# Sorted-table lookups in a fused two-layer kernel: one comparison and a difference product, table products in pieces, the own tile in one operation

## The chip, the cores and the metric

One core of one Trainium2 chip. The metric is device microseconds of one execution; the median of several runs is the time of a kernel. Engines are called as in the profile: PE (TensorE), PEld (its weight loads), DVE (VectorE), ACT (ScalarE), POOL (GpSimd), SP (SyncE, which issues most DMAs).

## What is computed

Two layers on x of shape 2 x 256 x 64 x 64, float32, so N = 4096 tokens per batch:

```python
# layer 0
e   = prelu(bn(conv3x3(x)))            # 64 channels
sim = e.T @ e                          # N x N per batch
p   = sparsemax(sim, rows)             # max(sim - tau, 0)
x   = x + x @ p
# layer 1 (256 channels in, 128 inside)
g = g_w x + g_b;  a = w_t theta(x);  b = w_p phi(x)
f = relu(a[:, None] + b[None, :] + c)  # N x N
y = (f / N) @ g
x = x + bn(wz_w y + wz_b)
```

Layer 1 needs no N x N matrix where the tokens are sorted. f(i, j) is not zero only for those j whose b_j lies above -(a_i + c). With the tokens of a batch sorted by key b, y_i is a_i times a running sum of g plus a running sum of b g, both taken at one place of the sorted table. So layer 1 becomes: rank the keys, scatter rows (g, b) by rank, form running sums, and for each token find its place and fetch one row.

## The kernel before, in words

The executed path is `sparse_path` (L191 on). Nearly all of it is written as tasks of a list scheduler, `Plan` (L94 on): a task has a cost for each engine that may run it, a rank, tasks it comes after, a latency, and buffers that it takes or frees (`Ring`, `Hold`). `run` emits, again and again, the task that can begin first; among those that would start without delay `pick` takes the lowest rank. So the order on every engine is fixed when the kernel is built, by costs, due times and the rank constants of L281 (`R0`, `K0`, `CH0` for batch 0's ranking, `R1`, `K1`, `CH1` for batch 1's, `BE` for the counting products, `RW0`/`RW1` for the rows, `LS` for the lists, `DB`, `A0`, `G0` and so on). Each engine, and SP's queue of DMAs, then works in that order.

Layer 0, for each batch: the convolution (PE, `cv_in`/`cv_out`, L363); a survey of sim in tiles (PE `sv` L476, L508, ACT L528, DVE `xbs` L524), which lists the rows with more than one entry; for these rows the thresholds (DVE `mq` L777, ACT `z` L797 and DVE `z` L799); and the update `av` (PE L836), added into x by DVE L843. For four of the blocks POOL first multiplies x by a mask (L831; a `tick` L826/829 stands ahead). Layer 1's g, b and a come from `project` and `project_in` (PE `g` L873, L899; DVE `ga` L879, L906, L910).

Layer 1 is the class `Ranked`, twice. Batch 0 (r0) ranks all 32 tiles of 128 tokens. Batch 1 (r1) ranks 24 tiles; the other 8 tiles' part is computed directly (ACT `f` L1512, PE `py` L1520, ACT `rest` L1531). Its steps:

- `keys` (L1000 to 1014, DVE): the key per token, with two spare bits for a lower and an upper bound.
- `spread` (L939): PE turns the key column to a row (`pt_k` L924), ACT copies (`row_k` L928), SP stores it (`rd_k` L932) and loads it into all 128 partitions (`kb` L944). The same is done with a in pieces (`rd_a`, `ab`; `a_of_0` L1456 to 1462 for batch 0).
- `above(t)`: the keys of all columns from tile t on against tile t's keys, on ACT (Sign, L1050) or DVE (is_gt with a sum, L1054). The 0/1 matrix `junk` feeds PE `below` (L1065 and L1076), which counts along partitions for the later tiles; `below_out` (L1087) copies a row of it and `bt` (L1093) turns it.
- `ties(t)` (L1101, DVE): equal keys in the own 128 x 128 tile with a lower index.
- `place` (L1115 to 1120, DVE): the rank of four tiles; first for tiles 0 to 15, then for the others. `scatter` (L1126, POOL): one indirect DMA per tile into the sorted table `sg` in DRAM.
- `load` (L1141, SP) brings the sorted table back as `tab0`, `tab1`, and (L1143, L1144) the first key of the next partition as `nxt`. `products` (L1150 to 1153, DVE) makes b g; `sums` (L1160, DVE) the running sums within a partition; `po` (L1164, PE) and `raised` (L1167, DVE) add what lies before; `stored` (L1173, SP) writes the table `tb`.
- Lookups, for 8 blocks of 512 tokens: `limits` (L1177 to 1179) and `segments`, two DVE comparisons (L1187, L1188) that give a one-hot matrix of the partition in which each token's place lies; `pk` (PE L1196) reads that partition's keys out; `counts` (L1205 to 1208, DVE) counts within it.
- `fetch` (L1213, POOL): one indirect DMA per tile of 128 tokens, 32 in each batch; 16 fit the buffer `r`. `taken`: DVE L1226, PE `yr` L1233, then `yT` (ACT L1238, DVE L1240 in batch 1), PE `pz` (L960), DVE `x` (L964), and SP's store of the output (L967).

`begin` (L1255) and `chain` (L1305) write these as tasks.

Of the kernel before, what the change touches and what calls it, by code (L numbers as in the profile page):

```python
# [8 lines left out]
F32 = mybir.dt.float32  # L9
BF16 = mybir.dt.bfloat16  # L10
# [9 lines left out]
P = 128  # L20
# [14 lines left out]
TINY = 2.0**-60  # L35
STEEP = 2.0**40
# [154 lines left out]
def sparse_path(ctx: ExitStack, tc, a, out, rows_i):  # L191
# [89 lines left out]
    DB, CV1, LS, RW0, SV1, RW1, A0, G0, A1, R0, K0, CH0, R1, K1, CH1, P1, P2, SP1, PY, PF, BE = -15.47, 6.58, -12.34, -12.34, -12.37, -24.38, 6.88, -11.7, -0.72, -32.06, -0.3, 11.42, 11.12, 11.73, 6.58, -24.23, -0.6, 10.82, 17.06, 12.47, -12.07  # L281
# [698 lines left out]
    class Ranked:  # L980
# [43 lines left out]
        def turn(self):  # L1024
            self.a = small.tile([P, 2, NT], F32, name=f"a_{self.b}", tag=f"a{self.b}")
            nc.scalar.copy(self.a[:, 0], self.ga[:, :, CI + 2])
            nc.scalar.mul(self.a[:, 1], self.ga[:, :, CI + 2], -1.0)
# [8 lines left out]
        def above(self, t, on_act, d):  # L1036
# [11 lines left out]
            c = ds(t * P, n - t * P)  # L1048
# [49 lines left out]
        def ties(self, t):  # L1098

            junk = small.tile([P, P], BF16, name=f"tied_{self.b}_{t}", tag="tied", bufs=1)  # L1100
            nc.vector.scalar_tensor_tensor(  # L1101
                junk, self.kb[:, ts(t, P)], self.key[:, t : t + 1], low,
                ALU.is_equal, ALU.mult, accum_out=self.cnt[:, t, 2:3],
            )

        def place(self, t0, bt):
# [5 lines left out]
            for t in range(t0, t0 + 4):  # L1112
                known = t * P - sum(u in self.on_act for u in range(t)) * (P // 2)
                known += (R - t) * P // 2 if t in self.on_act else 0
# [21 lines left out]
        def load(self):  # L1136
# [5 lines left out]
            self.nxt = small.tile([P, 1], F32, name=f"nxt_{b}", tag=f"nxt{b}")  # L1142
            nc.vector.memset(self.nxt, -3.0e38)  # L1143
            nc.sync.dma_start(out=self.nxt[0 : P - 1], in_=sv[1:P, 0, CI + 1 : CI + 2])  # L1144

        def products(self, h):
            b, R, tab = self.b, self.R, self.tab[h]
            if h == 0:
                self.kr = small.tile([P, R + 1], F32, name=f"kr_{b}", tag=f"kr{b}")
                nc.vector.tensor_scalar_mul(self.kr[:, R : R + 1], lane, float(R))  # L1150
            t0, n = self.parts[h]
            nc.vector.tensor_copy(self.kr[:, ds(t0, n)], tab[:, :, CI + 1])
            nc.vector.tensor_mul(
                tab[:, :, CI + 1 : CS], tab[:, :, 0:CI], tab[:, :, CI : CI + 1].to_broadcast([P, n, CI])
            )
# [19 lines left out]
        def limits(self):  # L1175
            self.lim = small.tile([P, 2], F32, name=f"lims_{self.b}", tag=f"lims{self.b}")
            nc.vector.tensor_scalar_mul(self.lim[:, 0:1], self.kr[:, 0:1], -1.0)  # L1177
            nc.vector.memset(self.lim[0:1, 0:1], -3.0e38)
# [773 lines left out]
```

## Time and profile before

Three runs: 744.95, 740.04 and 737.0 us, median 740.04. The profiled execution took 744.85 us, of which the span from the first to the last instruction is 743.1; the mean granted clock of PE was 0.894. All times below are of that execution.

| | |
|---|---|
| PE, DVE, ACT, POOL busy | 601.1, 527.4, 322.3, 221.8 us |
| batch 0: keys written, on all partitions (first `junk`) | 374.3 to 376, 391.9 us |
| batch 0: first and last scatter | 437.7, 488.4 us (end) |
| batch 0: `x_7_1` (last L843), table load issued | 498.9, 490.1 us |
| batch 1: key row on all partitions (first DVE `junk`) | 523.1 us |
| batch 1: first and last scatter | 564.9, 598.6 us (end) |
| batch 0: table raised, first fetch | 590.6 to 599.3, 609.9 us |
| batch 1: table raised, first fetch | 642.7 to 649.3, 657.6 us |
| last fetch ends, last `x`, end of the span | 708.2, 733.5, 743.1 us |

How to read it: a line with the mark L1101 is line 1101 of the kernel; `a<-b` is written tile and read tiles; "busy, mean ns" is the sum and the mean of one. Rows by stage give the window, its length, the busy time of PE, PEld, DVE, ACT and POOL with the number of instructions, the granted clock, the DMA share and GB/s. A wait is put down to what ended last before the waiting instruction.

### The profile page before, as it was taken

The numbers are of one execution on the slowest core, as the hardware profiler recorded it, in microseconds if no ns is written. First come the engines' busy times: TensorE is split into PE (matmuls) and PEld (weight loads), VectorE is DVE, ScalarE is ACT, GpSimd is POOL, SyncE is SP. The second block draws the span as 40 slices with busy tenths as digits, with TensorE's granted clock in tenths as the row PEclk, the third lists the DMA queues.
The fourth block names the chain that finished last, engine by engine and source line by source line (L and its number), as shares of the span: only waits on it lengthen the run. The fifth ranks groups of instructions, "written<-read, shape, count | busy, mean of one in ns | idle before, by whom it ended". The sixth has DMA issues, their size and how long they took to land.

```text
span 743.1 us, 8392 instructions
## 1 busy us (share of the span) xinstructions
PE 601.1 (81%) x2829; PEld 286.6 (39%) x2835; DVE 527.4 (71%) x1074; ACT 322.3 (43%) x484; POOL 221.8 (30%) x290
## 2 busy tenths in 40 slices
PE   5998999999597999999877878766998876574562
PEld 4663444444332333435432233336543433341220
DVE  6966777777869877877589987016798627973551
ACT  0123575766376564772089863001796650000000
POOL 0119910000030402010304246820004737567510
PEclk9999999999789899999998978679799897578796
DMA  9621000110210000000230000153310193476541
GB/s 351 198 54 30 1 15 14 29 22 9 86 27 0 1 0 1 0 1 2 76 147 4 1 21 23 54 133 133 125 29 29 44 336 91 156 253 183 160 169 62
DMA packets 34268, 57.07 MB, mean 77 GB/s; under 512 B 12942, under 2 KB 21000, under 8 KB 33192
## 3 DMA queue, kind: packets, MB, share of 16 engines
q1 hardware_dynamic: 28440, 42.72, 17.1%
q0 software_dynamic: 5344, 13.14, 6.4%
q10 hardware_dynamic: 432, 0.59, 0.3%
q8 instruction: 24, 0.39, 0.2%
q14 instruction: 28, 0.23, 0.1%
HBM read 32.67 MB, written 21.66 MB: 73 GB/s over the span
## 4 chain that ended last, share of the span: by engine, by line
PE 59%; DVE 25%; issue 6%; another core or an unknown queue 3%; DMA 3%; ACT 2%; POOL 0%; DVEq 0%; SPq 0%; ACTq 0%
PE sv L476 14%; PE av L836 9%; PE py L1520 8%; PE cv_in L363 6%; PE cv_out L363 6%; DVE mq L777 3%; PE pz L960 3%; DVE junk L1054 3%; DVE tied L1101 2%; DVE x L964 2%; PE g L873 2%; PE g L899 2%; PE bt L1093 2%; DVE xbs L524 2%
## 5 line engine op out<-in xcount | busy, mean ns | idle before, releaser
L528 ACT ACTIVATE sv<-sv,nthr 128x1024 f32<-128x1024 f32 (+1 forms) x133 | 131.2, 986 | 99.3 <-PE sv L508 47.9
L524 DVE TENSOR_TENSOR xbs<-sv,xbs 128x1024 f32<-128x1024 f32 (+1 forms) x120 | 130.7, 1089 | 37.3 <-PE sv L476 30.3
L476 PE MATMUL sv<-e 64*128 64x512 f32 x512 | 136.3, 642 | 5.8 <-ACT sv L528 4.4
L836 PE MATMUL av<-z,xbs 128*128 128x512 f32 x192 | 114.0, 716 | 17.4 <-DVE x L843 8.8
L1126 POOL DMA_INDIRECT sg<-ga,rank x56 | 55.5, 990 | 79.2 <-DVE rk L1118 55.8
L1213 POOL DMA_INDIRECT r<-tb,k x64 | 65.5, 1024 | 44.1 <-issue 15.8
L1050 ACT ACTIVATE junk<-kb,bound 128x2816 bf16<-128x2816 f32 (+26 forms) x39 | 69.9, 1799 | 16.7 <-PE below L1076 8.7
L476 PEld LDWEIGHTS sv<-e 64*128 64x128 f32 x512 | 45.6, 195 | 72.2 <-issue 42.8
L836 PEld LDWEIGHTS av<-z,xbs 128*128 128x128 f32 x192 | 37.9, 221 | 78.7 <-issue 55.2
L1520 PE MATMUL py<-f,ga 128*128 128x512 f32 x128 | 67.7, 671 | 0.2 <-issue 0.2
L1233 PE MATMUL yr<-ident,r 128*128 128x128 f32 x64 | 16.8, 342 | 48.0 <-DVE r L1226 34.2
L363 PE MATMUL cv_out<-v,wu 128*64 128x256 f32 (+1 forms) x384 | 49.1, 395 | 7.6 <-DVE v L325 7.6
L1238 ACT ACTIVATE yT<-yr 128x512 f32<-128x512 f32 x8 | 4.8, 597 | 109.6 <-PE yr L1233 68.2
L446 POOL TENSOR_TENSOR sq<-es 128x512 f32<-128x512 f32 x8 | 8.9, 1111 | 133.4 <-ACT es L437 111.0
L363 PE MATMUL cv_in<-v,wu 128*64 128x256 f32 (+1 forms) x384 | 46.6, 382 | 1.0 <-ACT c L374 1.0
L843 DVE SCALAR_TENSOR_TENSOR x<-av,b,x 128x512 f32<-128x512 f32 x32 | 23.7, 747 | 32.6 <-PE av L836 19.4
L964 DVE SCALAR_TENSOR_TENSOR x<-pz,s,x 128x512 f32<-128x512 f32 x32 | 23.1, 746 | 31.8 <-remote 14.3
L960 PE MATMUL pz<-yT,wz_sb 128*128 128x512 f32 x64 | 39.5, 745 | 5.3 <-issue 1.9
L1054 DVE TENSOR_SCALAR_CACHE_REDUCE junk<-kb,ga 128x2688 bf16<-128x2688 f32 (+13 forms) x17 | 40.5, 2381 | 4.1 <-PE below L1076 3.7
L1512 ACT ACTIVATE f<-ab,ga 128x1024 f32<-128x1024 f32 x32 | 35.9, 1141 | 13.0 <-PE py L1520 7.3
L363 PEld LDWEIGHTS cv_out<-v,wu 128*64 128x64 f32 x384 | 28.4, 141 | 31.5 <-issue 14.2
L1520 PEld LDWEIGHTS py<-f,ga 128*128 128x128 f32 x128 | 25.8, 214 | 29.0 <-issue 28.7
(217 smaller groups left out, 859.4 us busy)
## 6 DMA issues: line engine op xcount, KB each, us to landing
out<-x SPq DMA_DIRECT2D x32, 256.0 KB
tb<-tab SPq DMA_DIRECT2D x3, 2056.0 KB
x<-in_x SPq DMA_DIRECT2D x8, 512.0 KB
tab<-sg SPq DMA_DIRECT2D x3, 1040.0 KB
x<-in_x SPq DMA_DIRECT2D x4, 544.0 KB
e<-e SPq DMA_DIRECT2D x16, 128.0 KB
et<-es SPq DMA_DIRECT2D x16, 128.0 KB
mask<-kd SPq DMA_DIRECT2D x2, 1024.0 KB
```

Source lines behind the costliest of these rows:

```text
L363: nc.tensor.matmul(d[jp, g][ts(h, CR), n, (r0 - r) * HH : (r1 - r) * HH], lhsT=taps(j, kc, dy), rhs=v[:, kc, r0 + dy - 1 : r1 + dy - 1], s ...
L476: nc.tensor.matmul(ps[:, ts(h, CB)], lhsT=lhs(h), rhs=e[ts(h, CR), q], start=True, stop=True)
L524: nc.vector.tensor_tensor(out=acc[:, cols], in0=d[i, q][:, cols], in1=acc[:, cols], op=ALU.max)
L528: nc.scalar.activation(ps, ps, AF.Relu, bias=both["nthr"][:, i : i + 1], accum_out=got_s["over"][:, i, q : q + 1])
L836: nc.tensor.matmul(pss[j, ct], lhsT=got["xb"][:, k, ts(ct, P)], rhs=got["zs"][k][:, ts(j, CB)], start=(k == 0), stop=(k == KB - 1),)
L960: nc.tensor.matmul(d["z"][:, ct], lhsT=wz_sb[:, ts(ct, P)], rhs=d["y"], start=True, stop=True)
L964: nc.vector.scalar_tensor_tensor(xc, d["z"][:, ct], s1[:, ct : ct + 1], xc, ALU.mult, ALU.add)
L1050: nc.scalar.activation(slot[:, c], kb[:, c], AF.Sign, scale=STEEP, bias=self.bound[:, 1, t : t + 1], accum_out=cnt[:, t, 3:4],)
L1054: nc.vector.tensor_scalar(slot[:, c], kb[:, c], self.key[:, t : t + 1], None, ALU.is_gt, ALU.add, accum_out=cnt[:, t, 1:2],)
L1126: rows = nc.gpsimd.indirect_dma_start(out=self.sg, out_offset=bass.IndirectOffsetOnAxis(ap=self.rank[:, t : t + 1], axis=0), in_=self.ga[: ...
L1213: nc.gpsimd.indirect_dma_start(out=self.r[:, t % TH], out_offset=None, in_=self.tb, in_offset=bass.IndirectOffsetOnAxis(ap=self.k[:, t : t ...
L1520: nc.tensor.matmul(pys[q][:, ts(h, CB)], lhsT=ga1[0][:, m, 0:CI], rhs=f[0][:, m % 4, ts(h, CB)], start=(m == NR), stop=(m == NT - 1),)
```

## The change

1. Lookups. One DVE comparison of a against a single limit writes a bf16 0/1 matrix `seg` (ring of two). PE multiplies it by a constant bf16 matrix, identity minus shifted identity, so that each partition's row has the next one's taken off (`one_segment`); ACT copies the result to `oh` (`one_segment_out`). `limits` has one column, and `nxt` with its memset and DMA is gone; the keys kept for `pk` have their sign turned; the count is limited by a `min`.
2. Table products are tasks of four tiles each: on ACT four operations of 128 x 128, or on DVE one of 128 x 512. The keys are copied apart from them (`keys_of`).
3. `ties` becomes `own`: key difference above a tiny negative step for lower indices, one operation. `above` starts at the next tile, 128 columns fewer, and the last tile needs none.
4. `turn` is one ACT copy instead of two.
5. The rank constants have new values, so the scheduler writes another order.

```diff
-    DB, CV1, LS, RW0, SV1, RW1, A0, G0, A1, R0, K0, CH0, R1, K1, CH1, P1, P2, SP1, PY, PF, BE = -15.47, 6.58, -12.34, -12.34, -12.37, -24.38, 6.88, -11.7, -0.72, -32.06, -0.3, 11.42, 11.12, 11.73, 6.58, -24.23, -0.6, 10.82, 17.06, 12.47, -12.07
+    DB, CV1, LS, RW0, SV1, RW1, A0, G0, A1, R0, K0, CH0, R1, K1, CH1, P1, P2, SP1, PY, PF, BE = -27.4, 6.58, -13.63, -19.99, -13.75, -12.96, -8.26, -8.17, -0.45, -1.13, -0.3, 6.13, 6.58, -7.96, -7.87, -19.68, -8.17, 6.43, 17.29, 6.88, -7.87
...
-            self.a = small.tile([P, 2, NT], F32, name=f"a_{self.b}", tag=f"a{self.b}")
-            nc.scalar.copy(self.a[:, 0], self.ga[:, :, CI + 2])
-            nc.scalar.mul(self.a[:, 1], self.ga[:, :, CI + 2], -1.0)
+            self.a = small.tile([P, NT], F32, name=f"a_{self.b}", tag=f"a{self.b}")
+            nc.scalar.copy(self.a, self.ga[:, :, CI + 2])
...
-            c = ds(t * P, n - t * P)
+            c = ds(t * P + P, n - t * P - P)
...
-        def ties(self, t):
+        def own(self, t):
             nc.vector.scalar_tensor_tensor(
                 junk, self.kb[:, ts(t, P)], self.key[:, t : t + 1], low,
-                ALU.is_equal, ALU.mult, accum_out=self.cnt[:, t, 2:3],
+                ALU.subtract, ALU.is_gt, accum_out=self.cnt[:, t, 2:3],
             )
...
-            self.nxt = small.tile([P, 1], F32, name=f"nxt_{b}", tag=f"nxt{b}")
-            nc.vector.memset(self.nxt, -3.0e38)
-            nc.sync.dma_start(out=self.nxt[0 : P - 1], in_=sv[1:P, 0, CI + 1 : CI + 2])
...
+            nc.vector.tensor_scalar_mul(self.kr[:, ds(t0, n)], self.tab[h][:, :, CI + 1], -1.0)
+
+        def products(self, e, i):
+            tab = self.tab[4 * i // TH][:, ds(4 * i % TH, 4)]
+            if e == "A":
+                for t in range(4):
+                    nc.scalar.mul(tab[:, t, CI + 1 : CS], tab[:, t, 0:CI], tab[:, t, CI : CI + 1])
+            else:
+                nc.vector.tensor_mul(
+                    tab[:, :, CI + 1 : CS], tab[:, :, 0:CI], tab[:, :, CI : CI + 1].to_broadcast([P, 4, CI])
+                )
...
-        def segments(self, i, a):
+        def segments(self, i, a, d):
+            if not seg:
+                both = one.tile([P, 3, CB], BF16, name="seg", tag="wu")
+                seg.extend([both[:, 0], both[:, 1], both[:, 2, 0:P]])
+                nc.vector.tensor_copy(seg[2], ident)
+                nc.vector.tensor_sub(seg[2][:, 0 : P - 1], ident[:, 0 : P - 1], ident[:, 1:P])
+            d["g"] = seg[self.next % 2]
+            self.next += 1
+            nc.vector.tensor_scalar(d["g"], a, self.lim, None, ALU.is_gt)
+
+        def one_segment(self, i, d):
+            d["ps"] = ps_sim.tile([P, CB], F32, name=f"os_{self.b}_{i}", tag="sim")
+            nc.tensor.matmul(d["ps"], lhsT=seg[2], rhs=d["g"], start=True, stop=True)
+
+        def one_segment_out(self, i, d):
             oh = self.oh[i] = work.tile([P, CB], F32, name=f"oh_{self.b}_{i}", tag="wb")
-            nc.vector.tensor_scalar(oh, a, self.lim[:, 0:1], None, ALU.is_gt)
-            nc.vector.scalar_tensor_tensor(oh, a, self.lim[:, 1:2], oh, ALU.is_le, ALU.mult)
+            nc.scalar.copy(oh, d["ps"])
...
-            nc.vector.tensor_tensor(self.k[:, ts(i, 8)], kf, pk[:, :, R], ALU.add)
+            nc.vector.scalar_tensor_tensor(
+                self.k[:, ts(i, 8)], pk[:, :, R], float(R * P - R), kf, ALU.min, ALU.add
+            )
...
+            made = [
+                plan.task({"D": 0.75, "A": 1.36}, lambda e, i=i: self.products(e, i), rk + i / 100.0, [lims]) for i in range(R // 4)
+            ]
...
-                s = plan.task({"D": 1.29}, lambda i=i, ab=ab: self.segments(i, ab()), rk + 0.3, [lims] + loaded + ([s] if i else []), take=ho, free=let)
-                pk = plan.task({"P": 1.2}, lambda i=i: self.places(i), rk, [s] + ([pk] if i % 2 else []), take=None if i % 2 else hk, free=[ho])
+                s = plan.task(
+                    {"D": 0.52}, lambda i=i, ab=ab, d=d: self.segments(i, ab(), d), rk + 0.3, [lims] + loaded + ([s] if i else []),
+                    take=hg, free=let,
+                )
+                u = plan.task({"P": 0.3}, lambda i=i, d=d: self.one_segment(i, d), rk, [s] + ([pk] if i else []), take=hs, free=[hg])
+                u = plan.task({"A": 0.6}, lambda i=i, d=d: self.one_segment_out(i, d), rk, [u], take=ho, free=[hs])
+                pk = plan.task({"P": 1.2}, lambda i=i: self.places(i), rk, [u] + ([pk] if i % 2 else []), take=None if i % 2 else hk, free=[ho])
```

How the written order stands against the one before, as the two programs list their instructions: up to the survey of batch 0 it is the same. Of the products, 10 of 14 pieces are on ACT and 4 on DVE. Batch 0's keys come behind the last rows of batch 1 instead of ahead of them. All of POOL's masks stand ahead of the first scatter. In SP's queue the load of batch 0's sorted table (L1141), which waits for all of its scatters, stands ahead of batch 1's key row (`rd_k` L932, `kb` L944) in both orders. POOL's fetches are 24 of batch 0, 32 of batch 1, 8 of batch 0 (before: 28, 32, 4). Most `f` of batch 1 come later in ACT's list.

## The prediction
> **What bounds the kernel now.** I read the busy table, the chain of work that ended last, the busy time by stage, and then the queues one by one. The page:
>
> ```profile
> span 743.1 us, 8392 instructions
> PE 601.1 (81%) x2829; PEld 286.6 (39%) x2835; DVE 527.4 (71%) x1074; ACT 322.3 (43%) x484; POOL 221.8 (30%) x290
> PE 59%; DVE 25%; issue 6%; another core or an unknown queue 3%; DMA 3%; ACT 2%; POOL 0%; DVEq 0%; SPq 0%; ACTq 0%
> ```
>
> The chain is shared by PE and DVE; ACT, which takes over work here, is on it with 2%. An average does not price a stage, so I cut the second half at its milestones (busy us of PE, PEld, DVE, ACT, POOL, then granted clock):
>
> ```profile
> 376.30:399.65 23.35, 17.36 (x62) 6.40 (x59) 22.60 (x41) 23.30 (x24) 0.38 (x2) 0.93 0.30 114
> 399.65:437.70 38.05, 29.58 (x145) 10.13 (x146) 37.52 (x62) 28.58 (x22) 13.55 (x12) 0.91 0.00 0
> 437.70:490.10 52.40, 36.41 (x120) 16.75 (x120) 21.22 (x95) 12.92 (x25) 38.38 (x67) 0.77 0.13 41
> 523.14:564.30 41.16, 39.76 (x187) 19.11 (x187) 36.05 (x85) 32.92 (x34) 0.00 (x0) 0.91 0.15 46
> 657.62:733.50 75.88, 45.05 (x120) 21.10 (x120) 38.30 (x90) 2.98 (x5) 35.03 (x36) 0.78 0.51 158
> ```
>
> Both rankings are DVE stages: 37.5 of 38.05 us (batch 0) and 36 of 41 (batch 1). Between them POOL streams scatters. The last stage is bound by no engine's work: PE 45 of 76, POOL 35; it is gathers and hand-offs. The queues and prices:
>
> ```profile
> L1126 POOL DMA_INDIRECT sg<-ga,rank x56 | 55.5, 990 | 79.2 <-DVE rk L1118 55.8
> L1213 POOL DMA_INDIRECT r<-tb,k x64 | 65.5, 1024 | 44.1 <-issue 15.8
> ```
>
> ```profile
> 490.10 2.72 SPq L1141 DMA_DIRECT2D tab<-sg  x2
> 505.35 0.25 SPq L1144 DMA_DIRECT2D nxt<-sg  x1
> ```
>
> ```profile
> 407.21 2.13 POOL L831 TENSOR_TENSOR x<-x,mask 128x1024 f32<-128x1024 f32 x1
> 407.25 2.23 DVE L1101 SCALAR_TENSOR_TENSOR tied<-kb,ga,low 128x128 bf16<-128x128 f32 x1
> ```
>
> ```profile
> L1153 DVE TENSOR_TENSOR tab<-tab 128x2048 f32<-128x2048 f32 x3 | 6.9, 2292 | 0.1
> ```
>
> POOL issues one scatter or gather per 1.27 us. A `tied` takes 0.35 us, but 2.23 when it meets POOL's mask: about 1.9 us lost each, six times.
>
> The Trainium skill, "SBUF — State Buffer", section "Who interferes with whom", has a VectorE instruction with two SBUF inputs contend with a GpSimd one that reads SBUF, by an exclusive lock. That fits the pair above. `own` still has two SBUF inputs, so by the rule the 1.9 us stays; the sum uses the row.
>
> **The change, part by part.**
>
> *Lookups.* Removed on DVE: two comparisons of each of 16 blocks. L1187 is 16 x 0.484 = 7.7 us, L1188 16 x 0.751 = 12.0. The new comparison writes bf16, which no row shows at this shape: below by a 0.15 us row (L1177), above by L1054's 512 columns (0.743). I take 0.484, the same operation. So 12.0 us leave DVE (7.8 to 17.3). ACT gains 16 copies of PSUM 128x512: L437 0.587, L1238 0.597, so 9.5 us. PE gains 16 bf16 products; `below` of that size is 0.377 (6 us), an fp32 `py` 0.67 (10.7). Each lookup is now DVE, PE, ACT, PE. That hides in the drain, where eight lookups have 10 us of gathers each; without that cover it costs 16 x about 1 us (0.38 + 0.59). It also adds waits: the product takes one of three PSUM buffers that `py` and `below` use, and ACT's copy waits for the product with `f` and `junk` queued behind it. Before there was no such wait; a late product would hold `f`, so `py`, which nobody needs before the drain.
>
> *Products.* Old: 3 x 2.292 + 1.224 = 8.1 us on DVE. New: 10 of 14 pieces on ACT (40 operations 128x128) and 4 on DVE, by slope (2.292 - 1.224)/1024 ns = 0.69 each with 0.16 fixed: 2.8. DVE loses 5.3. ACT: bounded by 0.25 (L1026, 128x32) and 0.555 (L736, 128x256); its pitch in those rows is 0.15 to 0.40, I take 0.28: 11 us (6 to 22), 9 of them in batch 1's ranking. There ACT then has 15.4 of `junk` (15,232 columns by L1050's 0.834 ns, eight times 0.34) + 9 + 2 `f` + 1 copying before the first place, 28 us, under DVE's 34. At 0.40 it is 32, still under.
> The skill speaks against this: "ScalarE: Activation LUTs", section "Rules for kernel authors", puts multiplies on VectorE and gives 0.3 us per operation plus 0.83 ns per element, an estimate of 16 us for the 40. No run here shows a piece yet.
>
> *Own tile.* `above` loses 128 columns per tile (L1054 slope 1.042 ns: 0.133 us each, 17 DVE operations, 2.2 us; ACT 0.107 x 37 = 4 us). `own` costs what `tied` did, collisions too. `low` scaled: under 0.2 us, early. Limits, turn and `nxt`: 0.5 us of DVE and ACT, and two DMAs less on SP, of which the second held POOL's first gather (11.3 us waited there with the table store).
>
> DVE in all: -20 us. What it brings depends on order, since ranks change too.
>
> *Order.* (1) Up to about 180 us instructions are the same. Keys of batch 0 were written at 374.3, ahead of the last row reductions; now they come behind them, behind 22.6 us of DVE work that starts 1 to 3 us earlier. Key row to all partitions took 16 us (376 to 391.9) with 3 us queued; 12 to 13 without. So 391.9 becomes 411.5: **later by about 20**.
> (2) DVE then has, to the first place of batch 0: six `junk` with 18,304 columns (20.3), 16 `own` at 0.40 (6.4), collisions 3 or 4 x 1.9 (6.5), 7 or 8 `x` at 0.747 (5.6), two `below` (1.4), `z` and places (2.5): 43 us, and 1.5 of PE hand-off. First scatter 456, before 437.7: **+18**.
> (3) Scatters: before, 50.6 us, because places came late (last place 472.8). Now all masks are ahead and `x_7_1`, `g` beside: DVE work of the whole stage 62 us from 411.5 gives the last place at 475 to 481, ahead of POOL, so 32 x 1.275 = 40.8: last one 497, before 488.4: **+9**.
> (4) In SP's queue the load of batch 0's table stands ahead of batch 1's key row, before too; but then the projections ended later than the load (`g` L899 on the chain to 512.6, kb issued at 515.7), so the queue decided nothing. Now `x_7_1` comes at 473 to 478 and keys at about 488, and the queue decides: wait 1.7, issue 2.7, `rd_k` 3, `kb` 0.4 + 7.5 from issue to first use: 512 to 514; before, 523.1. **-9**.
> (5) Batch 1's ranking: eight `junk`, 16,512 columns (18.9), 24 `own` (9.6), three `below` (2.0), two lookups and their set-up (1.6), sums and places (2.3): 34.4, and 2 to 3 of waits; before 41.1, with nine lookups inside. First scatter 551.5, before 564.9: **-13**.
> (6) Rest of lookups and sums: 20 us of DVE against 26 with waits. Table raised at 574 (590.6); last scatter 583 (598.6): **-16**.
> (7) Store issue and wait took 19.3 us (590.57 to 609.88), in part batch 1's load and `nxt`; now 18 to 19. First gather 593: **-17**. Batch 1's table raised 623 (642.7), first of its gathers 638.5 (657.6): **-19**; two pieces of products on ACT beside `r`, two on DVE.
> (8) Forty gathers are left instead of 36: 40 x 1.27 = 50.8 against 45.7, inside 76 us of drain; so between 0 and +5 given back, I take 1. The end: **-18**.
>
> **Sum.** The profiled execution took 744.85 us (span 743.1): 744.85 - 18 = 727. It is 4.8 above the median of the runs, 740.04; so 722.
>
> **Rivals.**
> A, *the queue eats it*. Step 2 or 3 is worse: the clock falls from 0.91 to the next stage's 0.77 under the interleaved `av`, and PE's 52 us of work become 52 x 0.91/0.77 = 61. With a blocked `own` or two more, the first scatter comes at 466 to 474; step 4 passes each us on. Gain 0 to 8: 732 to 740.
> B, *late hand-offs vanish*. The chain holds three gaps put down to an unknown queue, 10.5 + 8.2 + 6.0 = 24.7 us, all where POOL streams. Re-planned, half may go: 12 more, 710. Against: POOL streams longer than before.
> C, *slower: SP's in-order queue alone*. Each us by which batch 0's last scatter comes late delays batch 1's key row, and with it all that follows. For: batch 1's keys are then ready and the queue alone decides, which it didn't before; SP issues in order, and batch 0's scatters got nothing shorter. Against: 474 is 18 us beyond step 2. It decides from a first scatter at 474 (no gain) and costs over 1% from 482; at 486 the end is 12 us later than before, 752.
> D, *the drain gives it back*. Steps 1 to 7 hold, but `f` moves behind the ranking: 24 of 32 pairs at 2.1 us of PE (4 records of 0.53) are 51 us from 552, to 603 and beyond, beside batch 0's lookups and finish; 12 us of the lead are lost: 734.
>
> **How the numbers follow.** Forecast 0.48 (own range 714 to 730), A 0.20, B 0.12, C 0.12, D 0.08. A measurement of this kernel tells about 1%, 7.4 us. Faster: forecast and B, and a little of D: 0.62. Same: A, the rest of D and the mild part of C: 0.25. Slower: 0.13. Range 706 to 744: forecast, A, D and most of B, 0.8. The bounds of unknown costs (comparison -5 to +4, ACT pieces up to +4 on the path) lie inside it.
>
> **What would show it.** `kb` of batch 0 at 405 to 416 and first scatter at 450 to 462 (steps 1, 2); scatter pitch 1.28 with no waiting between (3); `rd_k` right behind the table load, `kb` of batch 1 at 508 to 518 (4); 37 us to its first scatter (5); first gather near 593 (7); last stage 74 to 82 us (8). ACT pieces over 0.4 us or comparisons over 0.6 would correct the prices. I am wrong if batch 0's first scatter comes after 474, or the lead of step 7 isn't there at the end.

## The result, and the profile after

The changed kernel took a median of 767.33 us (762.0 to 772.59, four runs); the kernel before took 742.5 beside it (737.0 to 746.4, four runs). The ratio is 1.034, with an interval of 1.0231 to 1.0448. The forecast of 722 us, faster, was wrong in its sign.

One thing must be said ahead of all else, because no number below can be read without it: the kernel *before*, unchanged, took 740 to 743 us beside this measurement and beside two of the six later series of runs, and 709 to 711 us beside the other four. Every ratio here is made within one series, and each is marked **case 742** or **case 710**, by what the kernel before took there. The changed kernel took 767 in case 742 and 715 in case 710. A median here is that of all runs, and a ratio leaves out runs more than 1.5% above the fastest of their kernel; this matters only for `after_again` below, whose four remaining runs have a median of 761.4.

The page of the changed kernel (767.33 us; the profiled execution took 769.87), busy table and shares of the chain:

```profile
span 768.1 us, 8480 instructions
PE 608.1 (79%) x2851; PEld 292.0 (38%) x2851; DVE 514.6 (67%) x1065; ACT 332.5 (43%) x526; POOL 219.2 (29%) x290
PE 58%; DVE 20%; issue 7%; another core or an unknown queue 7%; DMA 4%; ACT 3%; DVEq 0%; SPq 0%; ACTq 0%; POOLq 0%
```

DVE did lose work, 527.4 to 514.6 us, and its share of the chain fell from 25% to 20%. What grew is the share that no engine's work accounts for, from 3% to 7%. Those steps, in the chain of the changed kernel (start, length):

```profile
462.68 10.18 another core or an unknown queue
...
575.87 3.23 another core or an unknown queue
583.32 9.92 another core or an unknown queue
...
681.31 20.10 another core or an unknown queue
...
713.74 2.50 another core or an unknown queue
...
718.19 5.79 another core or an unknown queue
```

and in the chain of the kernel before:

```profile
479.25 10.48 another core or an unknown queue
...
674.31 8.21 another core or an unknown queue
684.21 6.00 another core or an unknown queue
```

They add up to 51.7 us against 24.7. The difference, 27, is about the 25 us by which the span grew (768.1 - 743.1). That is bookkeeping of one execution each; the repeats below test it. The busy time by stage of the changed kernel (busy us of PE, PEld, DVE, ACT, POOL, then granted clock, DMA share, GB/s), cut at the same milestones as the prediction's table: ranking of batch 0, its scatters, ranking of batch 1, last stage:

```profile
408.34:450.14 41.80, 35.81 (x171) 12.05 (x169) 39.71 (x64) 33.71 (x26) 9.13 (x9) 0.92 0.00 0
450.14:510.72 60.58, 44.88 (x232) 30.32 (x231) 22.55 (x110) 11.05 (x27) 34.12 (x65) 0.75 0.18 54
529.60:564.85 35.25, 21.42 (x105) 7.62 (x105) 32.64 (x88) 30.41 (x57) 0.00 (x0) 0.64 0.08 30
668.30:758.40 90.10, 51.05 (x132) 23.82 (x131) 40.18 (x92) 4.16 (x7) 38.59 (x40) 0.73 0.45 139
```

Both rankings are still DVE stages (39.7 of 41.8 us, 32.6 of 35.3), and batch 1's became 6 us shorter, as predicted. Two stages in which POOL streams became longer, and no engine is busy throughout either: batch 0's scatters by 8.2 us (52.4 to 60.6), with DVE busy for 22.6 of it and PE for 44.9, and the last stage by 14.2 (75.9 to 90.1), with DVE at 40 and PE at 51. PE does more in both than in the kernel before (36.4 and 45.0), but in case 710 the same 232 PE operations beside the scatters fit into 40.7 us (the row of `after_third` below).

What such a stretch looks like, in the time order of the changed kernel's last stage (start, us, engine, line, tiles, idle before and what ended it):

```profile
687.80 0.77 PE L1253 MATMUL yr<-ident,r 128*128 128x128 f32 x5 [2.35 <-issue]
...
695.21 0.69 DVE L1260 SCALAR_TENSOR_TENSOR yT<-yr,rest 128x512 f32<-128x512 f32 x1 [6.55 <-issue]
...
701.43 0.60 ACT L1258 ACTIVATE yT<-yr 128x512 f32<-128x512 f32 x1 [24.28 <-remote]
```

PE has finished its transposes at 688.57. DVE, idle for 6.55 us, reads the first block of them at 695.21, 6.6 us later, and ACT the next at 701.43, 12.9 us later. Up to 698.5 POOL issues a gather every 1.26 us. Call it a **late result**: by its records PE is done, the reader is idle, and the hand-off has not arrived. The profile models the ends of matmuls, so this row alone can't tell a late hand-off from a late end; the series of hand-offs below can.

### The profile page after: what moved, and what is told of

Same layout as the page of the kernel before. It is cut to its first block, busy times and chain, and to the rows that moved or that the text cites. A ratio compares the mean times of both kernels' runs of the same rounds, so it can differ in the third digit from the quotient of the medians.

```text
span 768.1 us, 8480 instructions
## 1 busy us (share of the span) xinstructions
PE 608.1 (79%) x2851; PEld 292.0 (38%) x2851; DVE 514.6 (67%) x1065; ACT 332.5 (43%) x526; POOL 219.2 (29%) x290
## 4 chain that ended last, share of the span: by engine, by line
PE 58%; DVE 20%; issue 7%; another core or an unknown queue 7%; DMA 4%; ACT 3%; DVEq 0%; SPq 0%; ACTq 0%; POOLq 0%
PE sv L477 14%; PE av L837 10%; PE cv_out L364 6%; PE py L1551 6%; PE cv_in L364 5%; PE pz L961 3%; DVE mq L778 3%; DVE junk L1054 3%; PE g L900 2%; DVE x L965 2%; DVE own L1102 2%; DVE xbs L525 2%; PE bt L1093 1%; PE pk L1214 1%
## 5 line engine op out<-in xcount | busy, mean ns | idle before, releaser
L837 PE MATMUL av<-z,xbs 128*128 128x512 f32 x192 | 106.7, 680 | 13.5 <-DVE ga L880 9.1
L1233 POOL DMA_INDIRECT r<-tb,k x64 | 63.1, 987 | 58.0 <-DMA tb<-tab 19.2
L1050 ACT ACTIVATE junk<-kb,bound 128x2304 bf16<-128x2304 f32 (+24 forms) x33 | 58.8, 1784 | 41.3 <-remote 15.7
L477 PEld LDWEIGHTS sv<-e 64*128 64x128 f32 x512 | 45.5, 195 | 69.6 <-issue 40.6
L837 PEld LDWEIGHTS av<-z,xbs 128*128 128x128 f32 x192 | 36.1, 210 | 67.5 <-issue 52.1
L961 PE MATMUL pz<-yT,wz_sb 128*128 128x512 f32 x64 | 42.2, 787 | 20.9 <-DVE yT L1260 15.8
L1054 DVE TENSOR_SCALAR_CACHE_REDUCE junk<-kb,ga 128x2176 bf16<-128x2176 f32 (+17 forms) x21 | 45.5, 2172 | 17.4 <-DMA kb<-rd_k 10.2
L1076 PE MATMUL below<-junk,part_ones 128*1 128x512 bf16 (+3 forms) x214 | 27.6, 437 | 23.7 <-DVE junk L1054 14.7
L364 PEld LDWEIGHTS cv_out<-v,wu 128*64 128x64 f32 x384 | 28.8, 142 | 31.6 <-issue 14.2
L1258 ACT ACTIVATE yT<-yr 128x512 f32<-128x512 f32 x8 | 4.7, 596 | 73.1 <-remote 40.5
```

Source lines behind the costliest of these rows:

```text
L364: nc.tensor.matmul(d[jp, g][ts(h, CR), n, (r0 - r) * HH : (r1 - r) * HH], lhsT=taps(j, kc, dy), rhs=v[:, kc, r0 + dy - 1 : r1 + dy - 1], s ...
L477: nc.tensor.matmul(ps[:, ts(h, CB)], lhsT=lhs(h), rhs=e[ts(h, CR), q], start=True, stop=True)
L837: nc.tensor.matmul(pss[j, ct], lhsT=got["xb"][:, k, ts(ct, P)], rhs=got["zs"][k][:, ts(j, CB)], start=(k == 0), stop=(k == KB - 1),)
L961: nc.tensor.matmul(d["z"][:, ct], lhsT=wz_sb[:, ts(ct, P)], rhs=d["y"], start=True, stop=True)
L1050: nc.scalar.activation(slot[:, c], kb[:, c], AF.Sign, scale=STEEP, bias=self.bound[:, 1, t : t + 1], accum_out=cnt[:, t, 3:4],)
L1054: nc.vector.tensor_scalar(slot[:, c], kb[:, c], self.key[:, t : t + 1], None, ALU.is_gt, ALU.add, accum_out=cnt[:, t, 1:2],)
```

## The experiments

Four theories stood at the start: the order is worse (the rank constants), the lookups' four hand-offs are worse (DVE, PE, ACT, PE), the products on ACT are, or PE's results come late beside POOL's streams and the change only exposes more of them.

**Parts alone, case 710 (before: 709.46).** `new_ranks` is the kernel before with the new constants alone:

```diff
-    DB, CV1, LS, RW0, SV1, ... = -15.47, 6.58, -12.34, -12.34, -12.37, ...
+    DB, CV1, LS, RW0, SV1, ... = -27.4, 6.58, -13.63, -19.99, -13.75, ...
```

> The kernel before with only the rank constants of the changed one; its lookups, products, ties and above are the old ones. Theory A (the order is the loss: batch 0's keys behind the last rows, and stages shifted against POOL's streams): slower than before, 760 to 775 us, with batch 0's keys on all partitions at about 408 us as in the changed kernel. Theory B (the new lookup is the loss: two visits to PE instead of one while POOL streams): no change or faster than the changed kernel by more than 15 us, 735 to 750.

Measured: 724.75, ratio 1.022 (1.0171 to 1.027). `two_old` is the changed kernel with both comparisons back on DVE, and with the old constants:

> The changed kernel with lookups by two comparisons as before and with the old rank constants: of the change only own tile, trimmed above, product pieces and the single turn are left. Theory A: 728 to 742 us, since DVE has about 8 us less and the order is near the old one. Theory B: the same, 728 to 742. If it is slower than before by over 1%, one of the small edits costs by itself, and both theories are incomplete.

Measured: 761.83, ratio 1.072 (1.0673 to 1.0766). `two_cmp` is the same with the new constants:

```diff
+            oh = self.oh[i] = work.tile([P, CB], F32, name=f"oh_{self.b}_{i}", tag="wb")
+            nc.vector.tensor_scalar(oh, a, self.lim[:, 0:1], None, ALU.is_gt)
+            nc.vector.scalar_tensor_tensor(oh, a, self.lim[:, 1:2], oh, ALU.is_le, ALU.mult)
-            nc.vector.tensor_scalar(d["g"], a, self.lim, None, ALU.is_gt)
...
-            nc.tensor.matmul(d["ps"], lhsT=seg[2], rhs=d["g"], start=True, stop=True)
...
-            nc.scalar.copy(oh, d["ps"])
```

> The changed kernel with lookups by two DVE comparisons as before (12 us of DVE back, the 16 PE products and ACT copies out), with the new rank constants. Theory A: stays slow, 760 to 780 us. Theory B: 735 to 750, and the late PE results in the lookups (9.9 us before above, L1223, in the changed kernel) vanish.

Measured: 709.75, ratio 1.0007 (0.9985 to 1.0029). `first_half` is the changed kernel with the constants of the first half back, so that batch 0's keys come early again, as before, and with them its gathers go 27, 32, 5 (of batch 0, batch 1, batch 0) instead of 24, 32, 8:

```diff
-    DB, ..., LS, RW0, SV1, RW1, A0, G0, A1, R0, K0, CH0, ..., BE = -27.4, ..., -13.63, -19.99, -13.75, -12.96, -8.26, -8.17, -0.45, -1.13, -0.3, 6.13, ..., -7.87
+    DB, ..., LS, RW0, SV1, RW1, A0, G0, A1, R0, K0, CH0, ..., BE = -15.47, ..., -12.34, -12.34, -12.37, -24.38, 6.88, -11.7, -0.72, -32.06, -0.3, 11.42, ..., -12.07
```

> The changed kernel with the old rank constants for the first half (DB, LS, RW0, SV1, RW1, A0, G0, A1, R0, K0, CH0, BE), the new ones for batch 1 and the lookups. Batch 0's keys should come before the last rows again, on all partitions near 392 us. Theory A: 725 to 745 us. Theory B: 755 to 770.

Measured: 708.53, ratio 0.9983 (0.9959 to 1.0006). So constants and parts can't be judged apart: the new constants cost the old kernel 2%, and the old ones cost the changed kernel's other parts 7%. Why the second is so dear stands in POOL's time order of `two_old`:

```profile
577.77 0.97 POOL L1127 DMA_INDIRECT sg<-ga,rank  x1 [1.08 <-DVE rank L1121]
583.68 0.99 POOL L1221 DMA_INDIRECT r<-tb,k  x1 [4.94 <-ACT f L1526]
```

After a part of batch 1's scatters POOL goes over to batch 0's gathers, 32 of them, and comes back only then: the last scatter of batch 1 ends at 633.1, where the changed kernel in this case has it at 576 (`after_third`, below). None of the four chains held late results beyond 2.8 us (`two_old`), so the loss of 3.4% could not be looked for here.

**Repeats and two more parts, case 742 (before: 742.3).** `before_again` and `after_again` are unchanged:

> The kernel before, unchanged, for a profile beside the others on this chip. Theory A (late PE results are a matter of the chip or of the execution): the chain has no gap put down to an unknown queue if its time is near 709 us as beside the last four kernels, and about 25 us of such gaps if it is near 740. Theory B (they belong to the kernel's order): the same three gaps at any time.

> The changed kernel, unchanged, beside the kernel before. Theory A: where before takes about 709 us, the changed one has none of the late PE results, and what is left of the difference is what the prediction's steps gave without them: 690 to 715 us, a ratio of 0.97 to 1.01. Theory B: the ratio 1.034 of the first measurement stays.

Measured: 738.37 in a single run, with 28.6 us of late results on its chain; 767.82, ratio 1.0221 (1.0166 to 1.0276), with 34.0. `first_half_two` takes the early keys and the two comparisons together, `products_dve` puts all products on DVE:

> The changed kernel with lookups by two comparisons and the old rank constants of the first half: both single repairs together. If each cures a part of its own, 695 to 705 us where before takes 709; if the order on the later queues decides, no better than either (708 to 710).

```diff
-                plan.task({"D": 0.75, "A": 1.36}, lambda e, i=i: self.products(e, i), rk + i / 100.0, [lims]) for i in range(R // 4)
+                plan.task({"D": 0.75}, lambda i=i: self.products("D", i), rk + i / 100.0, [lims]) for i in range(R // 4)
```

> The changed kernel with all 14 product pieces on DVE (0.69 us each instead of four ACT operations). If the pieces on ACT hold up batch 1's ranking or the tables, 5 to 10 us faster than the changed kernel; if ACT has the room that the prediction gave it, the same within 4 us, or slower by up to 7.

Measured: 751.35, ratio 1.0124 (1.0081 to 1.0167), 23.0 us of late results; and 766.71, ratio 1.032 (1.0273 to 1.0367), 29.4. The products' place is not the cause: off ACT, the kernel is as slow. Without the new lookup and the late keys it is less slow, but which of the two counts in this case, these runs don't tell.

**The same kernel again, and the late results by themselves.** `after_third` is the changed kernel in case 710 (before: 710.43):

> The changed kernel, unchanged, a third time, for a chip on which the kernel before takes about 709 us instead of 742. Theory A (the late PE results come with the chip, and cost the changed kernel more than the one before): 695 to 712 us beside 709, no gap put down to an unknown queue, batch 0's first scatter near 451, batch 1's key row near 513, its first scatter near 547 to 552. Theory B (the order or the new lookup costs on any chip): 1.02 to 1.035 times before. If before takes about 742 again, the ratio is 1.02 to 1.035 by both.

Measured: 715.12, ratio 1.0063 (1.003 to 1.0097), and no step of its chain is put down to an unknown queue. So the same program takes 52 us more in the one case than in the other, and the kernel before 32. On the chains of case 742 late results hold 51.7 and 34.0 us of the changed kernel, 24.7 and 28.6 of the kernel before; in `after_again`, with the 34.0, the chain's "issue" is also larger (6.8% of 766.1 us, 52, against 5.3% of 709, 38). So most of what the cases differ by is late results; how much of the rest follows from them isn't settled. The record numbers the chip of each series: chip 10 had case 710 (`after_third`), then case 742 (`bench_again`), then case 710 again (`first_half_early`). If the number names one chip, the case doesn't go with the chip.

`bench` is the kernel before, with series of hand-offs behind all its work: four transposes on PE, a copy of the result by ACT, which releases the next four; once alone, and once beside each of several other loads.

```diff
+                for j in range(turns):
+                    nc.tensor.transpose(ps[:, j], state["y"][:, ts(j, P)], ident)
...
+                nc.scalar.copy(y, ps.rearrange("p t c -> p (t c)"))
...
+    hops("alone", 12, 4)
+    gate("g")
+    gathers(16)
+    hops("gather", 12, 4)
...
+    scatters(16)
+    hops("scatter", 12, 4)
```

> The kernel before with a series of hand-offs added behind its work, one after another; the output is the same. Each hop is four PE transposes, then an ACT copy that waits for them, which the next hop's transposes wait for; or a DVE copy and an ACT copy. Series: alone (12 hops), gather (12 hops beside 16 gathers on POOL), scatter (12 beside 16 scatters), vector (DVE and ACT beside 16 gathers), busy (as gather, with two more PE products per hop that wait for nothing), loads (12 beside four large loads by SP). Alone a hop should take about 1.5 us. Theory A1 (late PE results come from POOL's indirect DMAs): on a chip where before takes 742, hops of gather and scatter take 5 to 10 us, those of vector and loads 1.5 to 2; where it takes 709, all take 1.5 to 2. Theory A2 (they come from an idle PE at half clock, not from POOL): alone and loads are as slow as gather, and busy is quick. Theory A3 (they come from any DMA traffic): loads as slow as gather.

> The same series of hand-offs, for a chip on which before takes about 742 us. Beside 710 they all took 1.85 us per hop (DVE and ACT 1.1 to 1.25), so POOL's indirect DMAs delay nothing there. Theory A1 (on the other chip POOL's indirect DMAs hold up PE's results): gather and scatter 4 to 10 us per hop, alone, vector and loads as before. Theory A2 (an idle PE is slow there): alone, pause and calm as slow as gather, busy quick. Theory A3 (any DMA traffic): loads slow too. If before takes 710 again, 1.85 everywhere, and nothing is told apart.

`bench` ran in case 710, `bench_again`, the same program, in case 742 (before: 740.23). Time of one hop, us, read from the starts of ACT's copies:

| beside | case 710 | case 742 |
|---|---|---|
| nothing | 1.85 (first two 1.39) | 1.85 (first four 1.39) |
| 16 gathers | 1.85, all | 1.85, one of 4.15 |
| 16 scatters | 1.85, all | 1.85, then 2.78 and 4.91 |
| gathers, PE kept busy between hops | 2.16, first 3.74 | 2.16, first 4.26, then 4.96 and 6.37, then 1.84, 4.27 and 2.16 |
| plain loads | 1.85 (first two 1.39), one of 2.13 | 1.85 (first three 1.39), one of 2.13 |
| 16 gathers, hop from DVE to ACT | 1.11 to 1.26 | 1.11 to 1.26 |

Two late hops in ACT's time order of `bench_again`:

```profile
789.94 0.59 ACT L1571 COPY yscatter<-pscatter 128x512 f32<-128x512 f32 x1 [1.26 <-PE pscatter L1566]
792.72 0.59 ACT L1571 COPY yscatter<-pscatter 128x512 f32<-128x512 f32 x1 [2.20 <-PE pscatter L1566]
797.63 0.59 ACT L1571 COPY yscatter<-pscatter 128x512 f32<-128x512 f32 x1 [4.32 <-remote]
799.48 0.59 ACT L1571 COPY yscatter<-pscatter 128x512 f32<-128x512 f32 x1 [1.26 <-PE pscatter L1566]
```

and PE's of the one between:

```profile
793.36 1.11 PE L1566 MATMUL pscatter<-ident,yscatter 128*128 128x128 f32 x4 [1.67 <-ACT yscatter L1571]
```

PE ends at 794.47, ACT begins at 797.63: 3.2 us after it, where in a hop on time it is 0.1 (PE's end 789.85, ACT's start 789.94). The next hop is on time again; POOL issued its last scatter at 794.06. Of the row with a busy PE only 4.96 and 6.37 are late results. In the hops of 3.74, 4.26 and 4.27 PE itself was slow: its extra products took 3.52 to 3.62 us instead of 1.88, and ACT began 0.1 us after the transposes. The hop of 6.37, PE's rows and then ACT's:

```profile
850.48 0.66 PE L1566 MATMUL pbusy<-ident,ybusy 128*128 128x128 f32 x4 [1.82 <-ACT ybusy L1571]
850.98 1.88 PE L1570 MATMUL zbusy<-x,ident 128*128 128x512 f32 x4
...
856.21 0.59 ACT L1571 COPY ybusy<-pbusy 128x512 f32<-128x512 f32 x1 [5.78 <-remote]
```

PE had begun the products behind the transposes at 850.98, so it wasn't stuck on the transposes; ACT got their result 5.1 us after PE's end (851.14). In these series late results appear only in case 742, and beside POOL's gathers and scatters and not beside plain loads. They appear with a busy PE too (2.9 and 5.1 us late, against 2.4 beside the gathers and 1.0 and 3.2 beside the scatters), so an idle PE isn't needed for them. Whether DVE's results can be late as well these series don't tell: PE's first late one came 13 us or more after POOL's stream began, and the hops from DVE to ACT were over 12.8 us after theirs began (808.27 to 821.05). The kernels' own traces say more: in the views of what DVE and ACT waited for, of the kernel before and of the changed one in case 742, every wait put down to "remote" stands before an operation that reads a product of PE or reuses a buffer that PE frees, and none of PE's own waits is so marked. What in the chip holds the results up is open.

**What is left without late results.** In case 710 the forecast's -18 isn't there either. `early_gathers` takes three blocks of batch 0's gathers forward, so that 1 and not 8 of them stand behind batch 1's:

```diff
-                self.taken(i, rk, self.then["rest"])
+                self.taken(i, rk - 25 if self.b == 0 and i < 3 else rk, self.then["rest"])
```

> The changed kernel with one more rank: batch 0's first three output blocks are planned ahead of batch 1's table work, so 31 of batch 0's 32 gathers go before batch 1's instead of 24. Theory D (batch 1's table is raised 8.6 us earlier than in the kernel before, and the drain gives it back through eight gathers, 10 us of POOL, and batch 0's last blocks behind batch 1's): where before takes about 710 us, 700 to 708, 5 to 12 us less than the changed kernel. Where it takes about 742, 745 to 760. Rival (the tail is bound by PE at half clock whatever the order): within 3 us of the changed kernel, 712 to 718 beside 710.

Measured in case 742: 754.95, ratio 1.0176 (1.0135 to 1.0217), 34.2 us of late results. Then four versions side by side in case 710 (before: 710.45), the changed kernel once more among them:

> The changed kernel beside the next three on one chip, so that these can be set against it. Where before takes about 742 us: 755 to 770. Where it takes about 710: 711 to 718.

> Lookups by two comparisons again, all else as changed. Where before takes 742: if the second visit to PE in each lookup is what gathers more late PE results, 8 to 20 us below the changed kernel, with no late result ahead of a lookup's counts; if the order does it (ranking and output blocks beside POOL's stream), within 5 us of the changed kernel. Where before takes 710: 709 to 712, 3 to 6 below it, from the copies and hops alone.

> Old rank constants for the first half, new lookup. Where before takes 742: if the order does it, 8 to 20 us below the changed kernel and no 10 us gap in batch 0's scatters; if the lookup does it, within 5 us of the changed kernel. Where before takes 710: 707 to 711.

> 31 of batch 0's gathers ahead of batch 1's. Where before takes 710: 700 to 708 by theory D (5 to 12 below the changed kernel), 712 to 718 if the tail's order is nothing. Where before takes 742: 5 to 12 below the changed kernel by D, again within 3 otherwise.

Measured: 715.11, ratio 1.009 (1.0061 to 1.0119); 712.09, 1.0064 (1.0023 to 1.0105); 708.34, 0.9993 (0.9966 to 1.0021); 707.38, 0.9971 (0.9937 to 1.0005). So against the changed kernel two comparisons gain 3 us here (712.09; the lookup's hand-offs alone aren't isolated by this, since the gathers then stand otherwise: 22, 24, 8, 8, 2), the old constants of the first half 7 and the earlier gathers 8. The gathers' part is seen in the last stage. Stage windows from batch 1's raised table to the last `x`, of `after_fourth` and of `early_gathers_b`:

```profile
619.30:704.90 85.60, 66.54 (x191) 34.95 (x191) 50.66 (x103) 9.10 (x15) 42.56 (x44) 0.76 0.60 191
```

```profile
622.90:695.50 72.60, 56.16 (x176) 29.84 (x175) 47.52 (x99) 8.00 (x13) 37.91 (x39) 0.81 0.67 214
```

The stage is 13 us shorter with five POOL instructions fewer in it, and it begins 3.6 later: 9.4 us gained at the last `x`. Last, both together, and a repeat of the two comparisons (case 710, before: 710.85):

> The changed kernel with the old rank constants for the first half and batch 0's first three output blocks planned ahead of batch 1's table: both repairs of the order together, new lookup kept; gathers go 28, 32, 4. Where before takes 710: 700 to 706, faster than before by 1% at most if the two add up; 707 to 709 if the second has nothing left to repair (27 of batch 0's gathers go ahead already with the first alone). Where before takes 742: 735 to 752.

> Lookups by two comparisons, for the case that before takes 742 here: 745 to 752 if the second visit to PE gathers the late PE results (the changed kernel took 757 to 777), 757 to 770 if the order does. Where before takes 710: 709 to 714 again.

Measured: 708.0, ratio 0.9983 (0.9947 to 1.0019); 711.86, 1.0041 (1.0002 to 1.008). The two gains don't add up, and no version is clearly ahead of the kernel before.

## Why the prediction was wrong, point by point

The milestones, us from the start. The last two columns are free of late results; that of the kernel before is the main part of `bench`, which is its program.

| | forecast | before, 742 | after, 742 | before, 710 | after, 710 |
|---|---|---|---|---|---|
| (1) batch 0's key row in use | 411.5 | 391.9 | 408.3 | 391.2 | 408.5 |
| (2) first scatter | 456 | 437.7 | 450.1 | 437.0 | 448.7 |
| (3) last scatter of batch 0 | 497 | 488.4 | 507.2 | 484.4 | 489.4 |
| (4) batch 1's key row in use | 512 to 514 | 523.1 | 529.6 | 510.3 | 509.1 |
| (5) first scatter of batch 1 | 551.5 | 564.9 | 564.9 | 548.7 | 544.5 |
| (6) batch 0's table raised | 574 | 590.6 | 603.1 | 569.1 | 566.5 |
| (7) batch 1's table raised | 623 | 642.6 | 653.1 | 624.0 | 615.4 |
| (8) last `x` ends | 715.5 (733.5 - 18) | 733.5 | 758.4 | 698.3 | 699.4 |

Read the forecast beside the last column: without late results every step from (1) to (7) came 3 to 8 us *earlier* than forecast. That profile is of a quick run (710.74; the median is 715.12). `after_fourth` (716.37) has 409.1, 450.9, 491.4, 512.2, 546.2, 569.6, 619.3 and 704.9, still at or ahead of the forecast up to (7). As a plan of work the sum held up to there. What failed: it left the late results in the 744.85 us that it subtracted from and put none into the new stages from (3) on, so that step (4) booked a part of them as gain, and it sized step (8) too small.

- **Step (4), "then the projections ended later than the load (`g` L899 on the chain to 512.6, kb issued at 515.7), so the queue decided nothing", failed.** That was true of the one profile shown, in which the chain has a late result of 10.48 us from 479.25 on. Without it the kernel before also has batch 1's keys at 488.2 and its key row in use at 510.3. The lead of the new order is then 1.2 us, not 9 (in `after_fourth` there is none). The way from the last scatter to the key row was also longer than the sum had it: 19.7 us in case 710 (489.4 to 509.1) and not 15 to 17. SP's time order of the kernel before, in case 742, and of the same program in case 710 (the main part of `bench`):

```profile
490.10 2.72 SPq L1141 DMA_DIRECT2D tab<-sg  x2
...
513.41 0.29 SPq L932 DMA_DIRECT2D rd_k<-row_k  x1
```

```profile
485.89 2.59 SPq L1141 DMA_DIRECT2D tab<-sg  x2
...
499.63 0.29 SPq L932 DMA_DIRECT2D rd_k<-row_k  x1
```

  From the table's load to the key row's transfer it is 23 us in the first and 14 in the second. About 8 of the 9 us of step (4) were this: the baseline's own late results, booked as a gain of the new order. The prediction had priced that apart, as rival B, with 12 us and 0.12, and had it in the forecast unseen.
- **In case 742 the new order met late results where the sum had none: step (3), "scatter pitch 1.28 with no waiting between", and all behind it failed there.** The sum took 24.7 us of them as part of 744.85 and added the new stages with none. The loss goes with them: the same program is 25 us behind the kernel before in case 742 and 5 in case 710, where there are none. The changed kernel had 10.2 us at 462.7, while DVE and ACT waited on PE in the middle of batch 0's scatters. DVE's time order there:

```profile
472.91 0.75 DVE L844 SCALAR_TENSOR_TENSOR x<-av,b,x 128x512 f32<-128x512 f32 x1 [10.23 <-remote]
...
500.47 0.98 DVE L911 TENSOR_TENSOR ga<-g,gb_sb 128x786 f32<-128x786 f32 x1 [9.68 <-remote]
```

  The first holds the last scatters (step 3: 507.2 instead of 497), the second batch 1's keys (507.6). During the second PE itself came on slowly, up to the moment when DVE was released. PE's rows then, and a block of the same 24 operations in case 710 (`after_third`):

```profile
498.96 0.81 PE L900 MATMUL g<-gw_sb,x 128*128 128x131 f32 x3 [1.31 <-issue]
500.38 2.78 PE L900 MATMUL g<-gw_sb,x 128*128 128x131 f32 x12 [0.60 <-issue]
```

```profile
475.27 2.86 PE L900 MATMUL g<-gw_sb,x 128*128 128x131 f32 x24
```

  The block that took 2.86 us there took from 491.94 to 503.16 here, its first half alone nearly 8 us. So more than the hand-off is held up. So rival C's mechanism, SP's queue behind a late last scatter, did decide with them (the key row came at 529.6), but not from a late *first* scatter: that came at 450.1, far below the 474 from which C was to begin. (The chances don't add up here: "slower" has 0.13, more than the whole of C, 0.12, of which a part was put to "same".) Over half of the late results on the chain, 28.4 us, came in the last stage, 20.1 of them in one step at 681.3.
- **Step (8), "between 0 and +5 given back, I take 1", failed on size.** In case 710 the lead of 8.6 us at (7) is a lag of 1.1 at the last `x`: 9.7 given back (`after_fourth`: a lead of 4.7, a lag of 6.6, 11.3 given back). Four gathers more at 1.26 us are 5.0. The rest is the tail. The last gather and the last `x` of `after_third`, then of the kernel before in `bench`:

```profile
679.85 0.95 POOL L1233 DMA_INDIRECT r<-tb,k  x1 [0.30 <-issue]
L965 DVE SCALAR_TENSOR_TENSOR x<-pz,s,x x32: 734/748/752, 611.5 to 698.7; 128x512 f32<-128x512 f32 x32
```

```profile
683.60 0.96 POOL L1213 DMA_INDIRECT r<-tb,k  x1 [0.30 <-issue]
L964 DVE SCALAR_TENSOR_TENSOR x<-pz,s,x x32: 735/744/752, 620.3 to 697.6; 128x512 f32<-128x512 f32 x32
```

  From the one to the end of the other the changed kernel needs 19.5 us, the kernel before 14.7, since batch 0's last two blocks now come behind all of batch 1. `early_gathers_b` shows it by taking it away: -7.7 us in its series. That is rival D in its effect, "the drain gives it back"; its mechanism, `f` behind the ranking, has a small part: the last `py` began at 620.1 (605.5 in the kernel before), and after step (7) `py` is on the chain of `after_third` for 3.5 us. Nor did the lookups hide in the drain, as the prediction had it: from 624.0 to 643.4 that chain is PE's `pk`, `os` and `pz` in turn, and `two_cmp_b` is 3 us faster.
- **Steps (1) and (2) were right in kind, too high in size**: the key row came 17 later (20 forecast), the first scatter 12 (18). `first_half_b`, with the early start back (and 5 late gathers instead of 8), is 7 us faster (708.34 against 715.11).
- **Rival A's clock fell in step (3), and not in step (2).** Batch 0's ranking ran at a granted clock of 0.92 (the first row of the stages above). In its scatters the clock was 0.75 in case 742 (0.77 before, in the prediction's table), but 0.94 in case 710, though the same `av` stand between the scatters. So it fell where the late results are; which of the two brings the other isn't shown. The window of `after_third` from the first to the last scatter, with 0.94 in the clock's column:

```profile
448.70:489.40 40.70, 35.19 (x232) 24.72 (x231) 22.71 (x111) 10.85 (x25) 33.85 (x63) 0.94 0.27 78
```

- **The prices were near.** Groups of the changed kernel, shapes apart (busy us, mean ns, idle before):

```profile
L1206 ACT COPY oh<-os 128x512 f32<-128x512 f32 x16 | 9.2, 583 | 31.1 <-PE os L1202 15.5 <-remote 9.6 <-issue 6.0
L1198 DVE TENSOR_SCALAR seg<-ab,lims 128x512 bf16<-128x512 f32 x16 | 8.0, 514 | 3.1 <-PE os L1202 3.1
L1202 PE MATMUL os<-seg 128*128 128x512 bf16 x16 | 6.6, 422 | 0.7 <-issue 0.7
L1156 ACT ACTIVATE tab<-tab 128x128 f32<-128x128 f32 x40 | 12.3, 387 | 7.4 <-DVE kr L1150 7.4
L1158 DVE TENSOR_TENSOR tab<-tab 128x512 f32<-128x512 f32 x4 | 2.5, 683 | 0.0
```

  Forecast: 9.5, 7.7, 6, 11 and 2.8 us. The Trainium skill, "ScalarE: Activation LUTs", section "Rules for kernel authors", which keeps multiplies on VectorE, gave an estimate of 16 us for the 40. It agrees for one piece (387 ns in the row), but pieces overlap, and 40 hold ACT for 12.3; `products_dve` shows no loss from having them there. ACT's copies of `os` also waited 9.6 us for no engine's work ("remote" in the first row), a wait that has no counterpart where both comparisons are on DVE.
- **`own` costs what `tied` did**, as forecast:

```profile
L1102 DVE SCALAR_TENSOR_TENSOR own<-kb,ga,low x56: 335/352/2236, 413.9 to 557.0; 128x128 bf16<-128x128 f32 x56
```

  Median 0.352 us, at most 2.236: a collision with POOL's mask costs what it did, but three fell together instead of six, and the sum is 24.7 us against 30.4. DVE in all still lost 12.8 us and not 20. It took 21 of the `junk` operations (L1054, 45.5 us) where it had 17 (40.5), and the forecast had 2.2 less for them. And the keys of batch 0 now fall beside POOL's mask at 392.4: two operations on 128x32 (L1002, L1003) take 2.15 and 2.08 us there, where the same two took 0.18 and 0.22 in the kernel before with no mask beside them.

## What to carry to other kernels

Before a gain is booked, look what the path that is to be shortened consists of: a stretch of the chain in which no engine works and no transfer lands ("unknown queue") isn't work that a better order is sure to remove. Left in the baseline and out of the new stages, it is a hidden gain in the forecast; here the 24.7 us became 51.7. If a kernel's time differs by per cents from one measurement to another, compare the chains of both before explaining a change by either. And an order tuned by constants belongs to its kernel: change parts and constants separately, and look where the last transfers of a batch stand in the queue.

## What the runs showed of the hardware

- In case 742 a product of PE that was finished by its records reached an idle DVE or ACT up to 13 us late, where that could be told beside POOL's indirect transfers only, and once PE's own next operations came on slowly too; in case 710 the chains had none, or at most 2.8 us. Between the cases the kernel before differs by 32 us (742.5 against 710) and the changed one by 52 (767 against 715). In the series of hand-offs the first late one came 13 us or more after POOL's stream began.
- Open: what holds the results up; what decides the case (chip number 10 had both); and whether it is the new lookup or the new order that meets more of it: the version with two comparisons and the new order ran in case 710 alone, and `first_half_two`, with two comparisons and early keys, had a ratio of 1.0124.
- A DVE operation with one SBUF input and constants (L1002, 128x32) took 2.15 us when it met POOL's mask, and 0.18 in the kernel before, without a mask beside it. The prediction reckoned with collisions only for `own`, which has two inputs. The Trainium skill, "SBUF — State Buffer", section "Who interferes with whom", does name `tensor_scalar`, this operation's form, among those that can take the shared ports; this row agrees.
